# Hand-over from a GRU to an attention-gated GRU: the last weighted sums in feature slices, 16 features stored first

## The chip, the cores and the metric

The kernel runs on one core of one Trainium2 chip, as one program. A core has five engines with instruction streams of their own: TensorE (PE, matrix products), VectorE (DVE), ScalarE (ACT), GpSimd (POOL) and SyncE (SP, which here only issues DMAs). They wait for each other through semaphores. They work on SBUF; PE writes its results to PSUM, which DVE and ACT read too. DRAM is reached through 16 DMA engines. The metric is the device time of one execution in microseconds, median of several runs.

## The reference

For 1024 users with up to 100 past items each (128 numbers an item), the reference runs a GRU over the items, scores every state against a candidate item with a small MLP, and turns the scores into weights with a softmax over time. The weighted sum of the states is `pooled`. Its first 100 of 128 features are then taken, transposed, as attention weights of the 100 steps of a second recurrence, whose state at each user's last step enters a small prediction MLP.

```python
_, gru_seq = jax.lax.scan(gru_step, h0, jnp.swapaxes(item_historical_embedding, 0, 1))
keys = jnp.swapaxes(gru_seq, 0, 1)
...
feat = jnp.concatenate([keys, q, keys - q, q * keys], axis=-1)
score = _mlp(feat, [(att_W0, att_b0), (att_W1, att_b1), (att_W2, att_b2)], jax.nn.relu)
score = jnp.where(mask[:, :, None] == 1, score, -jnp.inf)
attn = jax.nn.softmax(score, axis=1)[..., 0]
pooled = jnp.einsum('bt,btd->bd', attn, keys)
att_seq = pooled.T[:T]
...
    u = a_t[:, None] * u
    h_new = (1.0 - u) * h + u * h_hat
```

So feature 0 of `pooled` weighs step 0 of the second recurrence, feature 1 step 1, and so on: the second recurrence can't take its step 0 before the softmax over all 100 scores is done, and for step t it needs feature t alone.

## The kernel before, in words

**Two phases.** `gru_phase` (from L199) runs the GRU on two halves of 512 users each, states as 128 features x 512 users. `augru_phase` (from L989) runs the second recurrence on the same users, now sorted by the length of their history, so that later steps have fewer columns. There are three builds of the second phase for different spreads of lengths. Between the phases stands a branch: each engine loads a register from `over_d` (L1475) and takes one of two nested `If`s (L1476, L1477). Within a phase the order of each engine's work is the order in which the code is written (`manual_schedule`); the tail of `gru_phase` (L912 to L987) and the head of `augru_phase` (L1396 to L1425) are laid out by hand.

**Attention MLP.** `attend(t)` (L691) scores step t-2 and earlier layers' steps in one go, with products of 32 columns that occupy parts of the array (`pack`, L700). `take(t)` (L724) adds the candidate item's own part `q0` on DVE (L734), applies relu on ACT (L739, or L741 with a bias) and sends the scores through an SBUF-to-SBUF DMA to `s_b` (L746), from which `softmax` transposes them (L786).

**Softmax and weighted sums in blocks.** The softmax is online: the steps are cut into blocks that end at `ENDS`, the last ones 93, 96, 98 and 100. For each block there are scores (L786, L790), maxima (L794 to L800), exponents on ACT (L806) and sums (L809 to L823, with `old` and `den` on L813 and L814). `Half.pool` (L617) then brings `pooled` up to date: it rescales it (L626), multiplies the states `kt` of each step of the block with their weights (L636) and adds the product (L637), at full width of 128 x 512, that is 16 groups of 32 users (`KH`) times 32 features (`R`) on 128 partitions. Half 0's sums run on POOL, half 1's last ones on DVE; the last block's sums run on DVE for both.

**Hand-over.** When the last block is in, DVE multiplies `pooled` with a mask `used` that is 0 where a user's history has ended (L978). The first 32 features go to `pooled_d[0]` in DRAM (L982), the other 96 to `pooled_d[1]` (L987 for half 1, on SP; L1402 for half 0, on ACT's queue). POOL gathers the 32 features back in the order of sorted users (`gather`, L153, four of 128 users for each half). PE transposes the gathered rows into one feature on all partitions (`weight_row`, L1053): feature 0 for `first_state` (L1064, L1065), feature 1 for `first_weights` (ACT copy on L1070). `store_weights` (L1076 to L1079) turns the gathered features into rows in DRAM, from which `load_att` (L1092) reads the later steps' weights.

**Work around it.** The states themselves go to DRAM too (`keys_d`, stored from `kt` on L609) and are gathered back in sorted order by POOL (`load_row`, L188; `gather_early` issues some of them in the GRU phase). `load_key` makes the second recurrence's inputs of steps 0 to 3 from them by transposes on PE (L1110) and ACT copies (L1111). `first_step` computes the gates of step 0 (matmul L1030, sigmoid and tanh L1032), `open_gates` (L1127) the input part of the gates of step 1, `close_gate` (L1131) the state part. In `half_step` follow the sigmoids (L1151, L1152), r times h (L1157), u times its weight (L1165), `rest` (L1168), tanh (L1139), its product (L1155) and the new state (L1159). PE's other work at the end of the GRU phase are the prediction's features (`features`, matmul L667, ACT copy L675, store L677).

The order of the tail just before the branch:

```python
        stage(2)
        exponents()
        stage()
        halves[0].pool(T, nc.gpsimd)
        halves[1].pool(T, nc.vector)
        gather_early(3)
```

The functions that the diff touches:

Of the kernel before, what the change touches and what calls it, by code (L numbers as in the profile page):

```python
# [57 lines left out]
AHEAD = 2  # L58

# [16 lines left out]
FREE_BANK, EARLY_BANKS, LATE_BANKS = 6, (2, 5, 6, 0), (3, 4, 1)  # L76
# [7 lines left out]
def kernel(ctx: ExitStack, tc: tile.TileContext, a: dict, out: bass.AP):  # L84
# [35 lines left out]
    inv_d = dram.tile([B, 2], I32, name="inv_d")  # L120
# [3 lines left out]
        dram.tile([B, n], F32, name=f"pooled_d{j}") for j, n in enumerate((R, P - R))  # L124
# [15 lines left out]
    idx = const.tile([P, GH, NH * 2], I32, name="idx")  # L140
    idx_k = const.tile([P, KH, NH], I32, name="idx_k")
    idx_p = const.tile([P, HB // PR], I32, name="idx_p")
# [8 lines left out]
    def gather(dst, src, g, i):  # L151

        nc.gpsimd.indirect_dma_start(  # L153
            out=dst,
            out_offset=None,
            in_=src,
            in_offset=bass.IndirectOffsetOnAxis(ap=idx[:, g, 2 * i : 2 * i + 1], axis=0),
        )
# [40 lines left out]
    def gru_phase(pools):  # L199
# [72 lines left out]
        def load_later():  # L272
# [31 lines left out]
            ids = pre.tile([P, NG, 2], I32, name="ids")  # L304
# [18 lines left out]
            nc.scalar.copy(own, ids[:, :, 0])  # L323
            room = []
# [114 lines left out]
            place_i = pre.tile([P, KH, NH, 2], I32, name="place_i")  # L439
# [12 lines left out]

            last = pre.tile([P, NK], F32, name="last")
# [31 lines left out]
        class Half:  # L485
# [131 lines left out]
            def pool(self, count, eng):  # L617

                while count and self.todo:
                    e, n, t = self.todo.pop(0)  # L620
                    count -= t is not None
                    acc = pooled[:, self.ks, :]
# [5 lines left out]
                    k = self.kt[t // G][:, :, t % G, :]  # L628
                    if t == 0:
                        eng.tensor_mul(acc, k, w)  # L630
                    else:
                        if psum:
                            d = blocked(banks["kw"])
                        else:
                            d = wp.tile([P, KH, R], F32, tag="kw", name="kw")
                        eng.tensor_mul(d, k, w)  # L636
                        eng.tensor_add(acc, acc, d)  # L637
                    if t is not None and t % G == G - 1:
                        del self.kt[t // G]


# [49 lines left out]
        def attend(t):  # L691
# [17 lines left out]

            for turn in range(2 * NH):  # L710
                i, j = divmod(turn, 2)
                for q in range(2):
                    first(i, q, j)
# [10 lines left out]
        def take(t):  # L724
# [6 lines left out]
            for half in halves:  # L731
                if t < T:
                    sums.append(wp.tile([P, HB], F32, name="f"))
                    nc.vector.tensor_add(sums[-1], p[half.i], q0[:, half.cols])  # L734
            for half in halves:
                half.mv = wp.tile([P, HB], F32, name="mv", bufs=4)
                to, of, bias = half.mv[rows, :], p[half.i][rows, :], bm[half.i][rows, :]
                if t < T:
# [19 lines left out]
        def softmax():  # L758
# [49 lines left out]
            def sums():  # L808
                nc.vector.tensor_mul(e[:, :, :n], e[:, :, :n], on)  # L809
                nc.vector.tensor_reduce(den_n, e[:, :, :n], AX.X, ALU.add)  # L810
                if j:
                    old = sp.tile([P, NK], F32, name="old")
                    nc.vector.tensor_mul(old, den_old, e[:, :, n])  # L813
# [120 lines left out]
        some(2, 3)  # L934
        take(T - 1)
        some(2, 3)
        attend(T)
        some(4)
# [3 lines left out]
        n = ENDS[-3] - ENDS[-4] + 1  # L942
        copy = banks["e"][0][:, : NK * n].rearrange("p (k n) -> p k n", n=n)
        nc.vector.tensor_copy(copy, weights[:, :, :n])
# [4 lines left out]
        halves[0].pool(T, nc.gpsimd)  # L949
        halves[1].pool(1, nc.vector)  # L950
        stage()
        take(T)
        some(4)
        attend(T + 1)
        some(5, 6)
        stage()
        take(T + 1)
        exponents()
        some(5, 6)
        some(7)  # L960
        for half in halves:
            half.store((T - 1) // G)
        halves[1].pool(T, nc.vector)
        stage()
        gather_early(3)
        halves[0].pool(T, nc.gpsimd)
        some(7)
        stage(2)
        exponents()
        stage()  # L970
        halves[0].pool(T, nc.gpsimd)
        halves[1].pool(T, nc.vector)
        gather_early(3)


        for half in reversed(halves):
            t = blocked(s_bs[NH * (soft["j"] % 2) + half.i])
            nc.vector.tensor_mul(t, later["used"][:, half.ks, :], pooled[:, half.ks, :])  # L978
            first, others = (
                d[half.cols, :].rearrange("(k r) (p c) -> p r k c", r=R, c=R) for d in pooled_d  # L980
            )
            nc.sync.dma_start(out=first[0], in_=t[:R])  # L982
            later["att", half.i] = [
# [5 lines left out]
    def augru_phase(pools, widths, alive):  # L989
# [420 lines left out]
        for i in range(NH):  # L1410
            load_key(3, i)
# [137 lines left out]
```

## Time and profile before

| | before |
|---|---|
| median of 3 runs | 2014.82 us (2014.07 to 2015.9) |
| profiled execution, its own time | 2014.8 us |
| span of the profile | 2013.0 us |
| granted TensorE clock, mean | 0.993 |
| PE busy | 1986.5 us |
| DVE busy | 1672.2 us |
| POOL busy | 1277.1 us |
| ACT busy | 935.5 us |
| DMA moved | 204.84 MB, 102 GB/s on average |

The span is the time from the first to the last instruction of the profiled execution, which is one execution and not the median. Busy times add up what each engine did; they overlap. The granted clock is the share of full speed at which TensorE was clocked. In lists of instructions, a number in brackets is the idle time before one, with what ended it; "issue" is time for which the profile shows no releaser. The GRU phase ends, and the second recurrence begins, between about 1376 and 1450 us of the span.

### The profile page before, as it was taken

To read this page: it belongs to the slowest core of one execution; us is meant where nothing else is said; L and a number is where in the kernel's file an instruction comes from. 1 tells how busy PE (TensorE), PEld (TensorE's weight loads), DVE (VectorE), ACT (ScalarE), POOL (GpSimd) and SP (SyncE) were. 2 spreads that over 40 slices of the span, in tenths; PEclk is the share of its full clock that TensorE was granted. 3 is DMA by queue.
4 is the path that set the end of the run, shared out by engine and by line. 5 is a ranking of instruction groups with operands and counts; after the bars stand their busy time and mean duration, and the time that the engine had idled before them with its cause. 6 is when DMAs were issued, how large, how long until landed. Compare 5 with 4: busy or idle time off the path is not lost.

```text
span 2013.0 us, 40935 instructions
## 1 busy us (share of the span) xinstructions
PE 1986.5 (99%) x15324; PEld 992.8 (49%) x15324; DVE 1672.2 (83%) x3017; ACT 935.5 (46%) x1679; POOL 1277.1 (63%) x1325
## 2 busy tenths in 40 slices
PE   9999999999999999999999999998899999999998
PEld 2345555555433333333333333334444556678997
DVE  7878999887978887888878898998487777888985
ACT  4444454454444454444444454453334444445553
POOL 0233939669796959595887868898674354445331
PEclk9999999999999999999999999999899999999998
DMA  4442333323334334333333333333343343333331
GB/s 124 98 117 91 107 103 103 92 83 104 115 112 102 120 107 121 115 112 102 111 98 96 107 104 94 107 96 106 102 127 101 97 110 98 93 105 95 85 78 30
DMA packets 242075, 204.84 MB, mean 102 GB/s; under 512 B 59506, under 2 KB 204890, under 8 KB 241866
## 3 DMA queue, kind: packets, MB, share of 16 engines
q1 hardware_dynamic: 227514, 169.37, 30.1%
q0 software_dynamic: 12480, 32.04, 5.7%
q8 instruction: 122, 2.00, 0.4%
q14 instruction: 87, 0.71, 0.1%
q10 hardware_dynamic: 1872, 0.72, 0.1%
HBM read 146.01 MB, written 54.41 MB: 100 GB/s over the span
## 4 chain that ended last, share of the span: by engine, by line
PE 95%; DVE 3%; issue 1%; ACT 1%; ACTq 0%; DVEq 0%
PE ps L534 49%; PE pm L700 17%; PE pr L1131 4%; PE ph L1131 4%; PE pu L1131 4%; PE pr L1127 4%; PE ph L1127 4%; PE pu L1127 4%; PE pr L1204 0%; PE ph L1204 0%; PE p L1324 0%; DVE pu L1155 0%; PE pu L1030 0%; PE pd L243 0%; DVE ps L564 0%
## 5 line engine op out<-in xcount | busy, mean ns | idle before, releaser
L534 PE MATMUL ps<-x,wih 128*32 128x512 f32 x4800 | 775.9, 593 | 0.0
L534 PE MATMUL ps<-hn,whh 128*32 128x512 f32 x4752 | 769.6, 592 | 1.4 <-ACT hn L582 1.4
L534 PEld LDWEIGHTS ps<-x,wih 128*32 128x32 f32 x4800 | 259.0, 110 | 302.0 <-issue 299.1
L534 PEld LDWEIGHTS ps<-hn,whh 128*32 128x32 f32 x4752 | 257.0, 110 | 298.7 <-issue 294.6
L519 POOL TENSOR_TENSOR xm<-x,m 128x512 f32<-128x512 f32 x200 | 236.7, 1183 | 142.2 <-DMA m<-mask_d 82.5
L546 ACT ACTIVATE r<-ps,brz 128x512 f32<-128x512 f32 x200 | 137.5, 688 | 388.4 <-PE ps L534 388.2
L520 POOL TENSOR_TENSOR hist<-hist,xm 128x512 f32<-128x512 f32 x200 | 257.9, 1289 | 15.7
L700 PE MATMUL pm<-hn,wk 128*32 128x512 f32 x1200 | 266.4, 592 | 0.1
L700 PE MATMUL pm<-kq,wkq 128*32 128x512 f32 x1200 | 265.8, 592 | 0.0
L188 POOL DMA_INDIRECT rows<-keys_d,idx_k x218 | 211.4, 970 | 81.4 <-POOL rows L187 46.7
L637 POOL TENSOR_TENSOR pooled<-pooled,kw 128x512 f32<-128x512 f32 x191 | 246.0, 1288 | 15.0
L636 POOL TENSOR_TENSOR kw<-kt,e 128x512 f32<-128x512 f32 x191 | 206.3, 1080 | 70.7 <-DVE e L809 70.6
L565 ACT ACTIVATE ps<-ps,bih 128x512 f32<-128x512 f32 x200 | 132.4, 662 | 225.9 <-DVE ps L564 225.9
L554 DVE SCALAR_TENSOR_TENSOR u<-ps,bhh,r 128x512 f32<-128x512 f32 x198 | 147.6, 746 | 73.2 <-PE ps L534 70.5
L1139 ACT ACTIVATE c<-ph,bh 128x510 f32<-128x510 f32 (+57 forms) x174 | 88.1, 507 | 258.8 <-PE ph L1131 221.3
L700 PE MATMUL pm<-mv,w 128*32 128x512 f32 (+1 forms) x808 | 196.3, 592 | 0.8 <-DVE e L790 0.8
L569 DVE TENSOR_TENSOR d<-hn,ps 128x512 f32<-128x512 f32 x198 | 136.1, 687 | 35.9 <-ACT ps L565 35.5
L570 DVE TENSOR_TENSOR d<-ps,d 128x512 f32<-128x512 f32 x200 | 138.3, 692 | 28.4 <-ACT ps L566 14.0
L187 POOL COPY rows<-rest 128x1 f32<-128x1 f32 x202 | 38.3, 190 | 193.0 <-DVE rest L1168 182.9
L582 ACT COPY hn<-ps 128x512 f32<-128x512 f32 x200 | 116.4, 582 | 92.8 <-DVE kq L576 91.0
L564 DVE TENSOR_TENSOR ps<-ps,u 128x512 f32<-128x512 f32 x200 | 140.0, 700 | 22.4 <-PE ps L534 1.5
L571 DVE TENSOR_TENSOR ps<-ps,d 128x512 f32<-128x512 f32 x200 | 139.9, 699 | 6.8
(228 smaller groups left out, 3120.4 us busy)
## 6 DMA issues: line engine op xcount, KB each, us to landing
x<-in_hist_x SPq DMA_DIRECT2D x210, 256.0 KB
keys_d<-kt SPq DMA_DIRECT2D x48, 1024.0 KB
m<-mask_d SPq DMA_DIRECT2D x200, 128.0 KB
rows<-keys_d,idx_k POOLq DMA_INDIRECT x218
s_b<-mv SPq DMA_DIRECT2D x200, 8.0 KB
keys_d<-kt SPq DMA_DIRECT2D x32, 64.0 KB
mask_i<-in_mask SPq DMA_DIRECT2D x8, 200.0 KB
part_d<-part SPq DMA_DIRECT2D x2, 400.0 KB
```

The source lines that it names most:

```text
L188: nc.gpsimd.indirect_dma_start(out=r[:, at, :], out_offset=None, in_=keys_d[q], in_offset=bass.IndirectOffsetOnAxis(ap=idx_k[:, k, i : i + ...
L519: nc.gpsimd.tensor_mul(d, x, m)
L520: nc.gpsimd.tensor_add(acc, acc, d)
L534: nc.tensor.matmul(p[ts(q, R), :], lhsT=w[:, g, ts(q, R)], rhs=v, start=(j == 0), stop=(j == len(parts) - 1),)
L554: nc.vector.scalar_tensor_tensor(out=u, in0=ph, scalar=bhh[:, 2:3], in1=r, op0=ALU.add, op1=ALU.mult,)
L564: nc.vector.tensor_add(pi, pi, u)
L571: nc.vector.tensor_add(pi, pi, d)
L636: eng.tensor_mul(d, k, w)
L637: eng.tensor_add(acc, acc, d)
L700: nc.tensor.matmul(p[i][s, :], lhsT=w[:, s], rhs=v, start=start, stop=stop)
L1127: nc.tensor.matmul(p, lhsT=m[:, 1, :], rhs=k, start=True, stop=False)
L1131: nc.tensor.matmul(p, lhsT=m[:, 0, :], rhs=v, start=False, stop=True)
```

## The change

`SOON = R // 2 = 16` is new: `pooled_d[0]` holds 16 features instead of 32, `pooled_d[1]` 112 instead of 96. The parts are:

1. The last block's sums (and, for half 1, those of the block before) are made in two slices, features 0 to 15 (`soon`) and 16 to 31 (`rest`), on all partitions. The `soon` slices come first, half 0's on POOL with one product on DVE (`product`), half 1's on DVE. They are stored at once from `pooled`, unmasked, half 1 by SP and half 0 by ACT's queue. Then DVE makes the `rest` slices of both halves and the multiplication with `used`.
2. The other 112 features are stored by SP in step 2 of the second recurrence, by four DMAs for each half.
3. The mask for the 16 early features is applied after the gather: a third column of `inv_d` carries each user's length in sorted order, `used_s` is made from it, and `first_state` multiplies 15 gathered features with it.
4. The keys of steps 0 and 1 and the gates of step 0 are made before the branch. The gates lie in `item` and in tiles of `s_b`, and the keys of step 0 and 1 in `h_all` and `hist`; the pool `fp3` goes. The keys of steps 2 and 3 are made within steps 1 and 2.
5. For the last two GRU steps the candidate item's part is added by PE, with six more products in each `attend` (`query`), and `take` reads PSUM directly.
6. For one softmax block the weights and `old` lie in PSUM while the sums are made (`soft["copy"]`).
7. In step 1 the copy of feature 1 (`first_weights`) stands behind the sigmoids.
8. The store of the last states to `keys_d` stands later on SP: behind the copies of scores for the last step and behind the second feature store. 13 rows of `keys_d` are gathered early instead of 14.

The diff, cut to its core:

```diff
+SOON = R // 2
...
-        dram.tile([B, n], F32, name=f"pooled_d{j}") for j, n in enumerate((R, P - R))
+        dram.tile([B, n], F32, name=f"pooled_d{j}") for j, n in enumerate((SOON, P - SOON))
...
-            def pool(self, count, eng):
+            def pool(self, count, eng, cs=slice(0, R)):
...
-                    acc = pooled[:, self.ks, :]
+                    acc = pooled[:, self.ks, cs]
+                    if n is None:
+                        eng.tensor_add(acc, acc, e)
+                        continue
...
+            def product(self, cs):
+
+                e, n, t = self.todo.pop()
+                d = wp.tile([P, KH, R], F32, tag="kw", name="kw")[:, :, cs]
+                w = e[1][:, self.ks, n].unsqueeze(2).to_broadcast(d.shape)
+                nc.vector.tensor_mul(d, self.kt[t // G][:, :, t % G, cs], w)
+                self.todo.append((d, None, t))
...
+            def query(i, *groups):
+                for q in groups:
+                    pack(i, q, wq[i], item[:, halves[i].cols], False, False)
+
             for turn in range(2 * NH):
                 i, j = divmod(turn, 2)
+                if j and T - 2 <= t < T:
+                    query(i, 0, 1)
+                    if i:
+                        query(1, QB[1])
+                        query(0, QB[0])
...
-                if t < T:
+                if t < T - 2:
...
+                f, old = e, None
+                if banks and both[1] is None:
+                    b = banks["e"][0]
+                    f = soft["copy"] = b[:, : NK * rows].rearrange("p (k n) -> p k n", n=rows)
+                    old = b[:, HB - NK :]
+                    nc.vector.tensor_copy(f, e[:, :, :rows])
+                nc.vector.tensor_reduce(den_n, f[:, :, :n], AX.X, ALU.add)
...
+        halves[0].pool(T, nc.gpsimd)
+        gather_early(2)
+        soon, rest = slice(0, SOON), slice(SOON, R)
+        late = [[], list(halves[1].todo)]
+        halves[1].pool(T, nc.vector, soon)
+        some(6, 7)
+        for half in halves:
+            key(1, half)
         for half in halves:
             half.store((T - 1) // G)
-        halves[1].pool(T, nc.vector)
-        stage()
-        gather_early(3)
-        halves[0].pool(T, nc.gpsimd)
-        some(7)
         stage(2)
         exponents()
...
         stage()
-        halves[0].pool(T, nc.gpsimd)
-        halves[1].pool(T, nc.vector)
+        for half in halves:
+            late[half.i] += half.todo
+        halves[0].product(soon)
+        halves[0].pool(T, nc.gpsimd, soon)
+        halves[1].pool(T, nc.vector, soon)
         gather_early(3)
-
-
+        for half, eng in zip(reversed(halves), (nc.sync, nc.scalar)):
+            eng.dma_start(
+                out=pooled_d[0][half.cols, :].rearrange("(k r) c -> r k c", r=R),
+                in_=pooled[:R, half.ks, soon],
+            )
         for half in reversed(halves):
+            half.todo = late[half.i]
+            half.pool(T, nc.vector, rest)
             t = blocked(s_bs[NH * (soft["j"] % 2) + half.i])
             nc.vector.tensor_mul(t, later["used"][:, half.ks, :], pooled[:, half.ks, :])
...
-                gather(r[:, g, :R], pooled_d[0], g, i)
+                gather(r[:, g, :SOON], pooled_d[0], g, i)
...
             nc.vector.tensor_mul(h3[i], p, h)
+            r = sorted_rows[i][:, :, 1:SOON]
+            nc.vector.tensor_mul(r, r, used_s[:, i, :, 1:])
...
-            if t == 1 and i == 0:
-                store_weights(0, pa.tile([P, HB], F32, tag="a", name="pw"))
-                first_state(1, spare)
-            elif t == 1:
-                first_weights(1, spare)
+            if t == 1:
+                first_weights(i, spare)
+                load_key(2, i)
...
             if t == 1 and i:
                 store_weights(1, spare)
+                load_key(3, 0)
+            elif t == 1:
+                open_state(1, 0)
+                store_weights(0, pa.tile([P, HB], F32, tag="a", name="pw"))
+                first_state(1, spare)
+            elif t == 2 and i == 0:
+                load_key(3, 1)
...
-        for i in range(NH):
-            load_key(0, i, (None, FREE_BANK)[i])
-        gates = [first_step(i) for i in range(NH)]
-        for i in range(NH):
-            load_key(1, i, (FREE_BANK, None)[i])
-        for to, t in later["att", 0]:
-            nc.scalar.dma_start(out=to, in_=t)
+        gates = [later["gates", i] for i in range(NH)]
+        keys.update({(1, i): later["key", 1, i] for i in range(NH)})
         sorted_rows = [gather_weights(i) for i in range(NH)]
-        for k in range(14, KH):
+        for k in range(13, KH):
             load_row(1, 0, k)
...
         open_gates(1, 1, EARLY_BANKS)
         open_gates(1, 0, LATE_BANKS)
...
-        first_weights(0, spare)
...
+                if t == FIRST[1] - 2:
+                    for to, of in later["att", i]:
+                        nc.sync.dma_start(out=to, in_=of)
```

## The prediction

> **What bounds the kernel now.** I read the busy totals and the chain that ended last first, then one table by stage. PE is busy 99% of the span and holds 95% of the chain, so a change away from PE's few pauses is worth nothing.
>
> ```profile
> span 2013.0 us, 40935 instructions
> PE 1986.5 (99%) x15324; PEld 992.8 (49%) x15324; DVE 1672.2 (83%) x3017; ACT 935.5 (46%) x1679; POOL 1277.1 (63%) x1325
> PE 95%; DVE 3%; issue 1%; ACT 1%; ACTq 0%; DVEq 0%
> ```
>
> The stage table (stretch, its length, busy time of PE, PEld, DVE, ACT, POOL, granted clock, DMA share, GB/s) shows where the pauses are.
>
> ```profile
> 1385.00:1400.00 15.00, 13.84 (x77) 8.51 (x70) 11.89 (x27) 7.44 (x16) 11.21 (x11) 1.00 0.25 78
> 1400.00:1420.00 20.00, 11.47 (x39) 6.37 (x38) 14.81 (x36) 6.73 (x11) 15.84 (x15) 0.74 0.63 170
> 1420.00:1440.00 20.00, 15.46 (x58) 8.10 (x57) 5.83 (x9) 4.72 (x8) 9.69 (x11) 0.92 0.19 40
> 1440.00:1460.00 20.00, 20.00 (x57) 9.66 (x56) 12.85 (x21) 7.89 (x12) 15.86 (x28) 0.99 0.62 185
> ```
>
> Here the GRU hands over to the second recurrence: PE stands idle 14 us in 55, and its clock drops to 0.74. All the edits lie between about 1376 and 1450. The timelines of DVE, POOL, ACT and PE (start, duration, instruction, idle before it and who ended it) give the links:
>
> ```profile
> 1388.35 1.29 DVE L734 TENSOR_TENSOR f<-pm,q 128x512 f32<-128x512 f32 x2 [2.55 <-PE pm L700]
> 1392.25 1.29 DVE L814 TENSOR_TENSOR den<-den,old 128x32 f32<-128x32 f32 x1
> 1402.27 0.19 DVE L814 TENSOR_TENSOR den<-last,old 128x32 f32<-128x32 f32 x1
> 1407.73 0.68 DVE L626 TENSOR_TENSOR pooled<-pooled,last 128x512 f32<-128x512 f32 x1
> 1414.71 1.29 DVE L978 TENSOR_TENSOR s_b<-used,pooled 128x512 f32<-128x512 uint8 x2
> 1429.23 0.70 DVE L1064 TENSOR_TENSOR first<-first,first_u 128x512 f32<-128x512 f32 x1 [13.22 <-PE first L1053]
> ...
> 1420.67 0.95 POOL L153 DMA_INDIRECT att_r<-pooled_d,idx  x1 [2.51 <-DMA pooled_d<-s_b]
> 1424.44 0.95 POOL L153 DMA_INDIRECT att_r<-pooled_d,idx  x1 [0.30 <-issue]
> ...
> 1432.73 0.58 ACT L1070 COPY at<-spare 128x512 f32<-128x512 f32 x1 [4.96 <-PE pu L1131]
> 1434.80 0.66 ACT L1151 ACTIVATE pr<-pr,br 128x510 f32<-128x510 f32 x1 [1.48 <-PE spare L1053]
> ...
> 1407.44 1.94 PE L1110 MATMUL pk<-ident,rows 128*128 128x128 f32 x8 [6.32 <-issue]
> 1427.83 1.16 PE L1053 MATMUL first<-ident,att_r 128*128 128x128 f32 x8 [0.72 <-issue]
> 1438.15 2.07 PE L1131 MATMUL pr<-h_all,wr 128*128 128x510 f32 x2 [0.37 <-DVE h_all L1065]
> ```
>
> The order is: last weighted sums on DVE until 1414.71, mask multiply until 1416.0, store, first gather 1420.67 (4.67 us after), fourth gather 1424.44, `first` at 1427.83, then step 1 with more waits. PE, before and after `first`, does what is there.
>
> [...] `pu<-k,wu` at 1411.16 takes 2.08 us where its like at 1420.05 takes 1.02, and the change comes after 5.2 us of work. [...] L814 takes 1.29 us at 1392.25, and 0.19 where one input lies in PSUM. [...]
>
> **The change part by part.** Times are in the clock of the profiled execution of before.
>
> *Query on PE for the last two GRU steps.* Four column groups work side by side; each holds four attend passes of 0.857 us (3.43 together, as from 1376.16 to 1379.59). Six extra passes make the fullest group six: 5.14, so +1.71 us twice. attend(98) ends at 1381.3 instead of 1379.59, two features (2.90) bring 1384.2, and attend(99) ends at E = 1389.4 to 1389.6 instead of 1387.24; its pauses of 1.3 us for `mv` go, since the `f` add on DVE (2x1.2) is gone. E is later by about 2.2 us.
>
> *DVE up to the last block's weights.* Gone: both pairs of `f` adds, and 2.31 - 0.4 = 1.9 us of L813/L814 through operands in PSUM. The full-width ops that stood behind them then fit before E + 3.0, when the scores return (store to `s_b` 1.66 to 2 us, plus relu). From there: two transposes and tops 3.05, exponents and sums 1.4, the other transposes 1.1, one half-width block of five ops 2.13, the next tops 3.05, and exp on ACT behind the key copies to about E + 15; sums, reciprocal and product end at X = E + 16.95 = 1406.5, against 1407.73. So 1.2 us of gain survive; the rest went into the later E.
>
> *Last sums in feature slices.* A full DVE op is 0.69 us and its 346-wide like 0.516, a slope of 1.06 ns an element: 256 wide is 0.42, and a block of five 2.13 instead of 3.48. After X: half 0's product 0.33, half 1's soon part 2.13, its rest (two blocks) 4.26, multiply 0.6, half 0's rest 2.13, multiply 0.7: 10.15 us, end at 1416.6. Before: 8.3 us, end at 1416.0. The full work is done once either way, in more and shorter instructions.
>
> *Early store and gather.* The store of half 1 could leave at X + 2.5 = 1409, half 0's after POOL's four half ops (2.4) at about E + 19.5 = 1409. But in the built program the first weight gather waits for DVE's last mask multiply: its tile takes memory that `used` held. PE's open_gates waits for the last rest op too (a PSUM bank). So the gather starts not behind the store but behind all the rest: 1416.6 + 0.1 = 1416.7, against 1420.67. What is saved is the landing and the POOL branch, 4.0 us. POOL itself (five full ops 5.75, two gathers 2.5, four half ops 2.4, three gathers 3.8, branch at most 2.5) is ready by E + 25.8 = 1415.3. One more rows gather (13 early instead of 14) follows the weights, with no one waiting.
>
> *Key stores moved.* 2 MB to keys_d now stand on SP directly in front of the pooled_d0 store. They take 264 to 360 GB/s in windows of 2 us of before, so with the other traffic 2.4 MB at 310 GB/s: 7.8 us from E + 16, drained at E + 24; the 16-feature store lands at E + 24.5 to 25 = 1414.5. The gather waits until 1416.7 anyway: cover of 2 us, cost nothing. Gone, it costs its lateness in full. The 112-feature store leaves at step 2; what hides it is the time until the later weights are gathered, well past step 15.
>
> *Keys and gates ahead of the branch.* Keys 0 and 1 and the four first gates run on PE while it waits for DVE, instead of 1407.44 to 1420. Before, open_gates (five us at full clock) ended at 1425.2 and keys 3 at 1427.1. Now it starts with DVE's last rest op at 1415.9, after some 8 us of idle[...]: six pairs of matmuls take 6.9 to 7.7 us, and event waits 0.7, ending 1423.5 to 1424.3. The fourth gather is issued at 1416.7 + 4.7 and lands two us later: 1423.4. Both meet, so `first` starts at 1423.7 to 1424.3 against 1427.83: -3.5 to -4.1 us.
>
> *From `first` to the steady steps.* ACT's copy of `at` (idle 4.96 before it, 1.48 after) comes behind the sigmoids, which frees 1.7 us on ACT; keys 2 and 3 transposed in steps 1 and 2 put four times 0.45 us on a busy PE. Walking both chains, ph of half 1 in step 1 comes 16.75 us after `first` instead of 17.0: -0.25.
>
> Sum: I take 1423.7[...]: -4.13 - 0.25 = -4.4, or a span of 2008.6 instead of 2013.0. The profiled execution was 2014.8 and the median 2014.82, so the same difference applies: **2010.5 us**. Own range of this case 2009 to 2012.
>
> **Rivals.** (a) *Slower: cold PE through step 1.* It speaks for it that PE now has idle stretches of 8 us before open_gates, and that the warm-up in before ran on gates that have moved away. If the pauses of step 1 keep the clock at half, the six gate pairs take 10.3 us, which puts `first` at 1426.6 (-1.2), and the eight matmul pairs of step 1 cost 0.86 us more each, of which some 5.5 us fall on the chain: +4.3, or 2019.1. [...] A pooled_d0 store that lands after 1421 behind the keys would have the same sign. (b) *Void part: ACT's stall stays or PE's extra 3.4 us delay E by more.* Before's DVE saw attend(99) 1.1 us after PE's modelled end; if that repeats E is 1390.5 and all behind it 1.0 later, and if ACT's 1.7 us do not come, step 1 costs 1.45 (the moved keys) instead of giving 0.25: -4.13 + 1.0 + 1.45 = -1.7, or 2013.1. (c) *More gain: clock high.* If the features and gates ahead keep the clock, open_gates ends at 1421.5, the gathers set `first` at 1423.4 (-4.4), and the half-clock pieces of step 1 in before (1.54 and 2.07 us instead of 1.02 at 1436.23 and 1438.15) give 1.5 more: -6.1, or 2008.7. That the gather is tied to the store, and goes before the rest, as the code's order suggests, would be more still; the built waits exclude it.
>
> **How the numbers follow.** Forecast 0.48, (c) 0.20, (b) 0.20, (a) 0.12. A difference of 0.2% (4.0 us) is about what a measurement of this kernel can tell from no change, so faster means below 2010.8, slower above 2018.8 (nearly all of (a)'s tail is counted there). Forecast lies on the bound: 0.33 of its 0.48 below, and all of (c): 0.53 faster; the rest of it and (b), 0.35 same; 0.12 slower. The range 2007.5 to 2014.5 holds nearly all of the forecast, (b) and (c), and leaves (a) and the outer tails out.
>
> **What would show it.** POOL's first gather near 1416.7, its releaser DVE's multiply and not a DMA; the DVE end near 1416.6; L813/L814 at 0.2 us in the first softmax; `first` near 1424 with half-clock gates ahead of it; ACT without the 4.96 us wait. Wrong if the gather follows a DMA landing later, if the clock stays low through step 1, or if E is later than 1390.5.

## The result, and the profile after

The changed kernel takes 2012.72 us (median of 14 runs, 2011.0 to 2015.82), the kernel before 2014.85 (14 runs, 2012.94 to 2016.83). The ratio is 0.9991, with a 95% interval of 0.9984 to 0.9998: about 2 us faster, where 4.3 were forecast. That holds for one chip: on another the order was the other way round, 2005.12 us before and 2007.45 after ("Second profiles" below). The profiled execution took 2012.06 us, its span is 2010.3.

First the totals and the chain that ended last, then the stage table (stretch, its length, busy time of PE, PEld, DVE, ACT, POOL, granted clock, DMA share, GB/s), all of the changed kernel:

```profile
span 2010.3 us, 40989 instructions
PE 1987.7 (99%) x15348; PEld 1198.2 (60%) x15348; DVE 1673.9 (83%) x3033; ACT 936.0 (47%) x1681; POOL 1273.8 (63%) x1325
PE 96%; DVE 1%; DMA 1%; issue 0%; ACT 0%; POOL 0%; SPq 0%; DVEq 0%; POOLq 0%; ACTq 0%
```

```profile
1385.00:1400.00 15.00, 15.00 (x90) 10.00 (x83) 13.68 (x38) 7.27 (x17) 13.23 (x13) 1.00 0.16 51
1400.00:1420.00 20.00, 13.93 (x35) 6.56 (x34) 11.74 (x33) 5.36 (x9) 12.20 (x15) 0.83 0.62 168
1420.00:1440.00 20.00, 15.52 (x58) 9.47 (x58) 9.07 (x15) 5.57 (x9) 12.11 (x17) 0.83 0.28 77
```

PE's pauses between 1385 and 1440 shrink from 14.2 to 10.6 us. But in 1420 to 1440 PE is no busier than before (15.52 against 15.46) at a lower clock (0.83 against 0.92). The gain lies before that stretch and part of it is lost within. The timelines of DVE, POOL, SP and PE (start, duration, instruction, idle before it and its releaser) show where:

```profile
1386.31 0.19 DVE L853 TENSOR_TENSOR den<-den,last 128x32 f32<-128x32 f32 x1
1404.27 0.41 DVE L662 TENSOR_TENSOR kw<-kt,last 128x256 f32<-128x256 f32 x1
1413.81 0.69 DVE L1056 TENSOR_TENSOR s_b<-used,pooled 128x512 f32<-128x512 uint8 x1
1422.53 0.70 DVE L1122 TENSOR_TENSOR first<-first,item 128x512 f32<-128x512 f32 x1 [8.03 <-PE first L1111]
1426.87 0.69 DVE L1217 TENSOR_TENSOR r<-h_all,pr 128x510 f32<-128x510 f32 x1 [2.79 <-issue]
1433.66 0.69 DVE L1123 TENSOR_TENSOR h_all<-spare,s_b 128x512 f32<-128x512 f32 x1
...
1415.87 0.95 POOL L155 DMA_INDIRECT att_r<-pooled_d,idx  x1 [4.57 <-DMA pooled_d<-pooled]
...
1406.75 3.54 SPq L1048 DMA_DIRECT2D pooled_d<-pooled  x1
...
1410.66 2.04 PE L1187 MATMUL pr<-hist,wr 128*128 128x510 f32 x2 [5.15 <-DVE last L652]
1421.90 0.49 PE L1111 MATMUL first<-ident,att_r 128*128 128x128 f32 x2 [0.72 <-DMA att_r<-pooled_d,idx]
1424.01 2.07 PE L1191 MATMUL pr<-h_all,wr 128*128 128x510 f32 x2 [1.62 <-DVE h_all L1123]
```

The start of the kernel differs by up to 2.7 us between executions of the same program, so stages are counted from the first product of attend(98) (1375.17 before, 1373.71 after). The two columns "again" are second profiles, taken on another chip, and are discussed below.

| us after attend(98) starts | before | before, again | after | after, again |
|---|---|---|---|---|
| attend(99) ends on PE | 12.07 | 12.05 | 13.50 | 13.50 |
| copy of the last block's weights ends | 32.64 | 31.62 | 30.64 | 30.48 |
| DVE's last mask multiply ends | 40.83 | 39.81 | 40.79 | 40.61 |
| first weight gather starts | 45.50 | 43.60 | 42.16 | 42.18 |
| DVE's first product of `first` | 54.06 | 52.12 | 48.82 | 48.94 |
| fourth tanh of the second recurrence | 80.94 | 75.38 | 78.97 | 78.34 |

From before to after, the first product comes 5.24 us earlier, but the way from there to the fourth tanh takes 30.15 us instead of 26.88. The difference, 1.97 us, is near what the timed runs show (2.13).

### The profile page after: what moved, and what is told of

Read it like the earlier page. It is cut to its first block, busy times and chain, and to the rows that moved or that the text cites. A ratio compares the mean times of both kernels' runs of the same rounds, so it can differ in the third digit from the quotient of the medians.

```text
span 2010.3 us, 40989 instructions
## 1 busy us (share of the span) xinstructions
PE 1987.7 (99%) x15348; PEld 1198.2 (60%) x15348; DVE 1673.9 (83%) x3033; ACT 936.0 (47%) x1681; POOL 1273.8 (63%) x1325
## 4 chain that ended last, share of the span: by engine, by line
PE 96%; DVE 1%; DMA 1%; issue 0%; ACT 0%; POOL 0%; SPq 0%; DVEq 0%; POOLq 0%; ACTq 0%
PE ps L547 51%; PE pm L723 18%; PE ph L1191 4%; PE pr L1191 4%; PE pu L1191 4%; PE pu L1187 4%; PE ph L1187 4%; PE pr L1187 4%; DMA rows<-keys_d,idx_k 1%; PE last L690 1%; PE pr L1269 0%; DMA item<-in_item 0%; PE ph L1269 0%; PE p L1389 0%; DVE pu L1215 0%
## 5 line engine op out<-in xcount | busy, mean ns | idle before, releaser
L547 PE MATMUL ps<-x,wih 128*32 128x512 f32 x4800 | 712.5, 593 | 0.0
L547 PE MATMUL ps<-hn,whh 128*32 128x512 f32 x4752 | 705.9, 592 | 1.3 <-ACT hn L595 1.3
L547 PEld LDWEIGHTS ps<-x,wih 128*32 128x32 f32 x4800 | 301.9, 110 | 225.7 <-issue 39.7
L547 PEld LDWEIGHTS ps<-hn,whh 128*32 128x32 f32 x4752 | 299.5, 110 | 222.5 <-issue 35.5
L653 POOL TENSOR_TENSOR pooled<-pooled,kw 128x512 f32<-128x512 f32 (+1 forms) x190 | 243.7, 1283 | 14.9
L652 POOL TENSOR_TENSOR kw<-kt,e 128x512 f32<-128x512 f32 (+1 forms) x190 | 205.6, 1082 | 67.9 <-DVE e L841 67.9
L723 PE MATMUL pm<-hn,wk 128*32 128x512 f32 x1200 | 245.5, 592 | 0.6 <-issue 0.6
L723 PE MATMUL pm<-kq,wkq 128*32 128x512 f32 x1200 | 245.5, 592 | 0.0
```

The lines of the kernel that those rows point to most:

```text
L547: nc.tensor.matmul(p[ts(q, R), :], lhsT=w[:, g, ts(q, R)], rhs=v, start=(j == 0), stop=(j == len(parts) - 1),)
L723: nc.tensor.matmul(p[i][s, :], lhsT=w[:, s], rhs=v, start=start, stop=stop)
```

## The experiments

Times are set against runs of the kernel before on the same chip, since it did not take the same time on all: 2013.13, 2011.58 and 2005.12 us in the three sets. Stages of profiles from different chips are compared with each other; the two profiles of the changed kernel differ by up to 0.2 us until the first product and by 0.6 at the fourth tanh.

**Is it the landing of the 16-feature store that holds the gather?** As I read the built program, POOL's first gather waits, in the branch that runs, for both stores to pooled_d0 and not for DVE; the run with early keys below bears that out. SP's issue of half 1's store takes 3.54 us at 1406.75, right behind 2 MB for keys_d. The DMA view of the changed kernel for 1413 to 1415 (packets, then each queue with packets, MB and share) still shows small packets on q1, of 64 bytes each by the store's pattern:

```profile
DMA packets 269, 0.09 MB, mean 46 GB/s; under 512 B 244, under 2 KB 252, under 8 KB 268
q1 hardware_dynamic: 230, 0.02, 9.3%
```

Counted in shorter windows, half 1's small packets begin at about 38.5 us after the start of attend(98), when the 2 MB ahead of them on the queue are through, and end at about 40.6; the gather follows at 42.2. Four runs try whether that is cause or coincidence. The first moves the key stores behind the early stores:

```diff
-        for half in halves:
-            half.store((T - 1) // G)
         stage(2)
...
                 in_=pooled[:R, half.ks, soon],
             )
+        for half in halves:
+            half.store((T - 1) // G)
```

> The changed kernel with one edit: the two 1 MB stores of the last states to keys_d are issued on SP behind the two pooled_d0 stores instead of in front of them. Theory 1 (landing): in the branch that runs, the first weight gather waits only for the two 32 KB stores, and half 1's lands at about 1415 because 2 MB stand in front of it on SP's queue. Then the gather starts where POOL's own branch lets it, 2.5 us after its last rows gather instead of 4.57, that is 2.1 us earlier; DVE's first product comes 1.5 to 2.1 us earlier and the kernel is 1.5 to 2 us faster (ratio to before 0.9981). Rival (POOL's branch or DVE's last multiply bound it): the idle time before the first weight gather stays at 4.2 to 4.6 us and the time stays within 0.5 us of the changed kernel.

Measured: 2012.77 us, ratio to before 0.9995 (0.9986 to 1.0003). The gather did not start earlier but later, at 42.91. POOL's timeline:

```profile
1415.79 0.95 POOL L155 DMA_INDIRECT att_r<-pooled_d,idx  x1 [5.46 <-DMA rows<-keys_d,idx_k]
```

SP's issue fell from 3.54 to 0.34 us and half 1's small packets were through by 35 us. But now half 0's store, issued by ACT, took longer: its 528 small packets (on q10) lay between 36.0 and 40.1 us, while the key packets were passing too, where they had taken from 37.6 to 39.7 in the changed kernel. The theory as I had put it, one queue and its order, is refuted. That the last landing counts, whichever store it is, fits but is not shown by this run: the gather comes 2.8 us after the last small packet, where it comes 1.2 to 1.9 us after it in the changed kernel and in the late-store runs below, and the profile names a gather of rows, some of whose packets passed as late as 42.5 us. The second run moves the key stores the other way:

```diff
         take(T + 1)
+        for half in halves:
+            half.store((T - 1) // G)
         some(4, 5)
...
-        for half in halves:
-            half.store((T - 1) // G)
         stage(2)
```

> The changed kernel with one edit: the two 1 MB stores to keys_d are issued on SP right behind the last copy of scores, some 4 us earlier, as in the kernel before. Theory 1 (landing): the 512 packets of 64 bytes of half 1's weight store are last seen 41 us after the start of attend(98) because 2 MB stand in front of them; now they are through by 37 us, and the first weight gather starts where POOL's branch lets it, at 40 us instead of 42.2, and DVE's first product comes 1 to 1.6 us earlier; time 1 to 1.5 us better than the changed kernel. Rival: the keys' traffic delays the scores of the last step or the features and with them the last softmax, which comes 0.5 us or more later, and the gain is gone.

Measured: 2006.96 us, ratio to before 0.9977 (0.9970 to 0.9984), on a chip where before took 2011.58. SP, POOL and DVE in its timelines:

```profile
1405.17 0.33 SPq L1048 DMA_DIRECT2D pooled_d<-pooled  x1
...
1411.50 0.95 POOL L155 DMA_INDIRECT att_r<-pooled_d,idx  x1 [1.77 <-DMA rows<-keys_d,idx_k]
...
1412.22 0.69 DVE L1056 TENSOR_TENSOR s_b<-used,pooled 128x512 f32<-128x512 uint8 x1
```

Both stores' small packets are through by 36 us, the gather starts at 39.23 (2.9 earlier than in the changed kernel), the first product at 46.55 (2.3 earlier), the fourth tanh at 76.69 (2.3 earlier). The last softmax copy is where it was (30.50). The gather now starts 0.72 us before DVE's last mask multiply, so it does not wait for it. Theory 1 held at these stages, with more than its figures. The changed kernel itself was not run on this chip, so the gain in time over it is not measured.

The third and fourth undo the early store, in the changed kernel and in the one with early key stores. Each half's features are stored from the masked tile, behind its rest sums:

```diff
-        for half, eng in zip(reversed(halves), (nc.sync, nc.scalar)):
-            eng.dma_start(
...
             nc.vector.tensor_mul(t, later["used"][:, half.ks, :], pooled[:, half.ks, :])
+            (nc.sync if half.i else nc.scalar).dma_start(
+                out=pooled_d[0][half.cols, :].rearrange("(k r) c -> r k c", r=R),
+                in_=t[:R, :, soon],
+            )
```

> The changed kernel with the early store undone: each half's 16 features are stored from the masked tile, so only when its rest sums and its mask multiply are done; everything else stays. Theory 1 (landing behind the keys): in the changed kernel the early store of half 1 lands only 41 us after the start of attend(98) because of the 2 MB in front of it, so the early start is mostly wasted: the late store (DVE's end is at 40.8, half 0's store lands at about 43) costs just 1.5 to 2.5 us at the first weight gather (43.5 to 44.5 instead of 42.2) and 1 to 2 us of time. Rival (the early store is worth the whole 5.8 us by which it is issued ahead of DVE's end): 4 us or more.

> The same undoing of the early store, with the key stores moved early as in the run that did that alone. There the first weight gather started at 39.2 us and DVE's first product at 46.6. Now the store can't land before about 43, so the gather starts at 43.5 to 44.5 and the first product 4 to 5 us later than in that run; the time is 3 to 4.5 us worse than there. Rival (the gain of that run came from relief of DMA traffic alone, not from an earlier landing): within 1 us of it.

Measured, on one chip with the changed kernel again (2007.45 us, 20 runs): 2009.32 us with the late store, 2009.58 with late store and early keys. The gathers start at 44.21 and 44.12, the first products come at 51.15 and 51.07:

```profile
1417.06 0.95 POOL L155 DMA_INDIRECT att_r<-pooled_d,idx  x1 [6.79 <-DMA pooled_d<-s_b]
```

```profile
1417.12 0.95 POOL L155 DMA_INDIRECT att_r<-pooled_d,idx  x1 [6.70 <-DMA pooled_d<-s_b]
```

With a late store it makes no difference where the keys stand (0.09 us at the gather, 0.26 us in the time). So the gain of the early keys is not relief of DMA traffic: it is the earlier landing. And the early store, as it was made, is worth 2.0 us at the gather and 1.9 us of time; with the keys out of its way it is worth 4.9 us at the gather (44.12 against 39.23, profiles of two chips).

The place of the key stores also moves PE's pause at the branch. The first product of open_gates with the keys behind, and with early keys:

```profile
1406.04 1.09 PE L1187 MATMUL pr<-hist,wr 128*128 128x510 f32 x2 [1.51 <-DVE pooled L653]
...
1407.20 1.09 PE L1187 MATMUL pr<-hist,wr 128*128 128x510 f32 x2 [3.27 <-DVE pooled L653]
```

PE's pause is 1.51 us in the one, 3.27 to 3.60 in the three runs with early keys, and 4.50 to 5.17 in the seven profiles with the keys where the changed kernel has them. In all 14 profiles PE's first product behind the branch starts 1.51 to 1.65 us after a packet of 16 KB on q8 has passed (1.59 us in the profile of before, 1.57 in that of the changed kernel), a queue that the DMA view calls "instruction". What PE waited for there, and why the packet comes later in some orders than in others, is not shown.

**Is it POOL's branch?** The three rows gathers ahead of the branch go behind the weights:

```diff
         halves[1].pool(T, nc.vector, soon)
-        gather_early(3)
...
-        for k in range(13, KH):
+        for k in range(10, KH):
```

> The changed kernel with one edit: the three rows gathers that POOL issues ahead of the branch are issued behind the eight weight gathers (10 early instead of 13). Theory 1 (landing): POOL reaches its wait 3.8 us earlier and waits 3.8 us longer, the first weight gather stays at about 11.5 us behind the last softmax copy, nothing changes in the time (within 0.5 us), unless step 4's rows come too late. Rival (POOL's branch): the gather starts 3.8 us earlier, and the time falls by about 2 us.

Measured: the first weight gather starts 11.53 us after the last softmax copy, as before this edit (11.52), though POOL had been idle 8.24 us. POOL's branch does not hold it. But the time rose to 2022.01 us (4 runs, ratio 1.0041, 1.0026 to 1.0057), which neither theory had. The DVE timeline shows where:

```profile
1440.03 0.68 DVE L1137 COPY att_t<-pw 16x512 f32<-16x512 f32 x1 [9.58 <-remote]
```

Its operand `pw` was complete on PE at 1432.94 by the profile. But the profile models when PE's products end, and the trace also records each semaphore event, the signals for which engines wait. PE's signals stop at 1431.51 and go on at 1437.14, 1438.57 and 1440.00, and the copy starts 0.03 us after the last of these. So DVE waited for a signal of PE that came about 7 us after the modelled end. Whether PE's products were late or only their signals, and why, is left open.

**Does the query on PE pay?**

```diff
-                if j and T - 2 <= t < T:
+                if False:
...
-                if t < T - 2:
+                if t < T:
```

> The changed kernel with one edit: the six extra products in each of the last two attends are taken out and the candidate's part is added on DVE again, as before. Theory 1 (the query pays): PE's two attends shrink by 1.7 us each, but DVE gets its two pairs of additions back (2.4 us) ahead of and inside the first softmax; the last softmax copy comes 0.5 to 1.5 us later and the kernel is 0.5 to 1.5 us slower than the changed one. Rival (PE's 3.4 us sit on the chain): the last softmax copy comes about 2 us earlier, and the kernel is 1 to 2 us faster.

Measured: 2013.91 us, ratio 1.0005 (0.9997 to 1.0013). attend(99) ends at 12.35 us instead of 13.50, but the last softmax copy comes at 33.18 instead of 30.64, the fourth tanh at 81.15 instead of 78.97. By these stages the query is worth 2.2 to 2.5 us, more than either theory gave it. The two profiles are of different chips, and the changed kernel was not timed on this one.

**Step 1: the clock, the order, or ACT?** First PE is kept busy while it waits for the gathers, with products into a bank that is overwritten next:

```diff
-        def weight_row(t, i, p):
+        def weight_row(t, i, p, turn=None):

             for g in range(GH):
+                if turn:
+                    turn(P)
+                    turn(P)
...
-        def first_state(i, p):
-            weight_row(0, i, p)
+        def first_state(i, p, turn=None):
+            weight_row(0, i, p, turn)
+            for _ in range(3 if turn else 0):
+                turn(2 * P)
...
```

> The changed kernel with one edit: while PE waits for the gathered weights, it makes products that nobody reads (two of 128 columns ahead of each of the four transposes of first, three of 256 behind them) into the bank that is overwritten next. Theory 1 (clock): step 1 takes 18.4 us from DVE's first product to the second half's ph because PE runs at half clock from 1424 to 1430; kept busy, pr and pu of step 1 take 1.02 us instead of 2.07 and 1.91, and the stretch shrinks by 2 to 3 us (ratio to before 0.998). Rival (order): the loss comes from what stands ahead of ph on PE (eight transposes for the weights and four for key 2) and from ACT's late copy; then pr and pu are short but the stretch shrinks by under 1 us, or the extra products delay first by what the clock gives back.

Measured: 2014.13 us, ratio 1.0009 (1.0000 to 1.0017). PE and ACT in its timelines:

```profile
1422.58 1.12 PE L1196 MATMUL pr<-h_all,wr 128*128 128x510 f32 x2 [0.89 <-issue]
1423.54 1.02 PE L1196 MATMUL pu<-h_all,wu 128*128 128x510 f32 x2
...
1426.03 0.66 ACT L1216 ACTIVATE pr<-pr,br 128x510 f32<-128x510 f32 x1 [21.86 <-PE pk L1175]
```

The products run at full clock now, 1.12 us instead of 2.07. But ACT takes `pr` up only at 1426.03, 2.3 us after its modelled end and 0.08 us after a signal of PE at 1425.95: a late signal again. The way from the first product to the first tanh grows from 8.95 to 9.44 us, that to the fourth from 30.15 to 33.42. Since late signals fell into the stretch, the run does not say what the half clock costs alone.

Then half 1's first state is put ahead of key 2:

```diff
             if t == 1:
                 first_weights(i, spare)
-                load_key(2, i)
+                if i:
+                    load_key(2, i)
+                else:
+                    first_state(1, pa.tile([P, HB], F32, tag="a", name="first"))
...
                 store_weights(0, pa.tile([P, HB], F32, tag="a", name="pw"))
-                first_state(1, spare)
+                load_key(2, 0)
```

> The changed kernel with one edit in step 1: half 1's first state (its eight transposes on PE and its two products on DVE) is put directly behind half 0's copy of feature 1, and half 0's key of step 2 behind the row store, so that the state of half 1 no longer waits for the copies of feature 1 and key 2 on ACT. Theory 1 (order of step 1): between half 0's r (1426.87) and half 1's state (1434.36) the changed kernel takes 7.5 us where before took 2.6, because the transposes stand behind key 2 and two copies in the same banks; the stretch then shrinks by 2 to 3 us, and the time by 1 to 2.5 us against the changed kernel (ratio to before 0.9985 or less). Rival (PE's half clock or late gathers set it): the stretch from DVE's first product to the fourth tanh shrinks by under 0.7 us and the time stays.

> The changed kernel with both edits, the key stores early and half 1's first state early. If both places are on the chain, their gains add up: the fourth tanh comes 3 to 4.5 us earlier after the start of attend(98) than in the changed kernel, and the ratio to before is 0.997 or less. If only one of them is on the chain, the result is that of the better one alone.

Measured: 2012.58 us (ratio 1.0004, 0.9998 to 1.0011), and with early keys as well 2009.00 (0.9989, 0.9982 to 0.9995), where early keys alone had 2006.96 on the same chip. Half 1's state is complete 10.0 us after the first product instead of 11.8, but the second tanh comes 21.82 us after it instead of 19.50: key 2 now waits for the bank that the row store empties. PE's timeline of the run with that edit alone:

```profile
1432.07 0.60 PE L1136 MATMUL pw<-ident,att_r 128*16 128x128 f32 x4 [2.08 <-DVE att_r L1125]
1434.02 0.93 PE L1170 MATMUL pk<-ident,rows 128*128 128x128 f32 x4 [1.36 <-DVE att_t L1138]
```

A wait took the place of the one removed; the expected 1 to 2.5 us did not come. With early keys as well the second tanh comes 19.76 us after the first product, where early keys alone had 19.49, so there too nothing is gained.

Last, the late copy of feature 1 alone, in the kernel before:

```diff
-        first_weights(0, spare)
...
             if t == 1 and i == 0:
+                first_weights(0, spare)
                 store_weights(0, pa.tile([P, HB], F32, tag="a", name="pw"))
                 first_state(1, spare)
```

> The kernel before with one part of the change alone: half 0's copy of feature 1 stands behind the two sigmoids of step 1 on ACT, and its transposes behind the state products on PE. The prediction has it free 1.7 us on ACT: r of half 0 comes 1.5 to 2 us earlier after DVE's first product, ph of half 0 too, and the kernel is about 1 us faster than before (0.9995). Rival [...]: the sigmoid starts no earlier than 5 us after DVE's first product, and the time is that of before within 0.5 us.

Measured: 2011.70 us against 2011.58, ratio 1.0004 (0.9995 to 1.0012). The expected gain is not there. r of half 0 does come earlier, 3.3 us after the first product instead of 6.3, but it comes after 3.3 us in the second profile of before too, without this edit. Half 1's state, which needs the bank that the copy frees, is complete after 8.94 us (8.86 before). The fourth tanh, at 79.26 us against 80.94, would have suggested a gain of 1.7 us that the times do not show.

**Second profiles.** Both kernels once more, on another chip:

> The changed kernel once more, for a second profile: if the stages are steady, gather at 42.2 +- 0.3, first product at 48.8 +- 0.5 and fourth tanh at 79.0 +- 0.7 us after the start of attend(98).

> The kernel before once more, for a second profile: if the stages are steady, gather at 45.5 +- 0.5, first product at 54.1 +- 0.7 and fourth tanh at 80.9 +- 0.7 us after the start of attend(98); if the fourth tanh comes near 79.3, the gain seen with half 0's late copy of feature 1 is no gain.

Measured: the changed kernel's stages repeat within 0.7 us (last column of the table). The kernel before does not: its fourth tanh comes at 75.38 instead of 80.94, and it takes 2005.12 us (median of the set's 40 runs) where the changed one takes 2007.45 (20 runs). On this chip the change is slower, ratio 1.0012 (1.0006 to 1.0019). Before is 1.0 us earlier there at the last softmax copy already and 1.9 at the gather, so the change gains 3.18 us up to the first product instead of 5.24, and loses 6.14 us after it instead of 3.27. PE's and ACT's timelines of before there, and PE's line in the first profile of before:

```profile
1424.30 1.06 PE L1053 MATMUL spare<-ident,att_r 128*128 128x128 f32 x8
1425.40 0.58 ACT L1070 COPY at<-spare 128x512 f32<-128x512 f32 x1 [2.14 <-PE spare L1053]
1427.24 0.66 ACT L1151 ACTIVATE pr<-pr,br 128x510 f32<-128x510 f32 x1 [1.26 <-PE pr L1131]
...
1428.82 1.06 PE L1053 MATMUL spare<-ident,att_r 128*128 128x128 f32 x8
```

Here the copy starts 0.04 us after its operand (`spare`, 1424.30 + 1.06 on PE). In the first profile the modelled end of the operand is 1429.88 and the copy starts at 1432.73, 2.85 us later. The semaphore events of that trace say why: PE's signal comes at 1432.71, and its next nine signals come together, between 1434.77 and 1435.10; the sigmoid starts at 1434.80. So ACT's 4.96 and 1.48 us of idle time were waits for late signals of PE, and no cost of the order in the code. In the second profile the stretches that follow are shorter too: half 1's state is complete 6.25 us after the first product instead of 8.86, PE's clock stays at 1.00 from 1420 to 1440, and the second tanh comes 13.05 us after the first product instead of 16.67.

In the four profiles on this chip all but at most one of PE's signals are on record, and between 1390 and 1450 us none comes over 0.1 us after the modelled ends. In each of the ten other profiles some come later than that in step 1, and 154 to 192 of about 2240 are not on record. Whether this makes the difference in time between the chips, and whether the recording itself has a part in it, is not shown; early keys took 2006.96 us on a chip with late signals.

## Why the prediction was right or wrong

The time was inside the range of 2007.5 to 2014.5 and the direction right on the chip of the result. But the size was half of the forecast, outside the narrower range of 2009 to 2012, and it came about as a sum of two errors that went against each other, which is luck. The number is nearly that of rival (b), 2013.1, by another sum.

- **Query on PE.** Forecast: E, the end of attend(99), 2.2 us later. Measured: 1.43. Each attend takes about 5.3 us, near the 5.14 worked out. The second grew by 0.55 us, with its pauses gone, but the first by 0.90 instead of 1.71, because its passes ran partly beside the last GRU products.
- **DVE up to the last weights.** Forecast 1.2 us earlier (31.3 us after the start of attend(98)), measured 2.0 (30.64). L853 takes 0.19 us as expected, beside POOL's product at 1386.29. (The prediction's own example at 1402.27 stands where POOL was idle; the like at 1406.64, beside a product on POOL, takes 0.19 us too. The runs show 0.19 us with an operand in PSUM against 1.29 us at 1392.25, and not what makes the difference.)
- **Sums in slices.** Forecast 10.15 us from the last copy to DVE's end, measured 1404.35 to 1414.50, that is 10.15. "The full work is done once either way" holds for both engines together only: in the kernel before, half 0's last block ran on POOL (1408.67 to 1414.50 in its timeline, not on DVE as stated at the top), and its second slice is new on DVE.
- **Early store and gather.** The start was near (41.5 us after attend(98) forecast, 42.16 measured) for the wrong reason. The step that failed is "in the built program the first weight gather waits for DVE's last mask multiply". With early keys the gather starts before that multiply, so the program does not hold it there. (As I read the built program, the wait stands in one of the three builds of the second phase, and not in the one that runs.) The gather follows the landing of the stores, and the step that then counts is the price of the moved key stores, put at "cost nothing": half 1's store landed at about 40.6, not at 39, with no cover from DVE. By its own sign, "its releaser DVE's multiply and not a DMA", the prediction failed here. What came true is what rival (c) named and excluded, a gather tied to the store, together with rival (a)'s late landing behind the keys, at a smaller price.
- **Gates.** open_gates was to start with DVE's last rest op (40.7 us); it started at 36.95, after 5.15 us of pause at the branch, at half clock for 5.2 us (2.04, 1.91 and 1.91 us for its first three pairs, 1.02 for its last two), as long as in the profile of before. The shorter stretch on which the forecast's 1423.7 rested was my estimate. So the wait for the last rest op did not hold its start. With the keys behind, where PE came earlier, its last pair did wait 1.76 us for DVE's rest op. It was done by 45.2, and `first` was bound by the gathers alone: 5.24 us of gain at the first product instead of 3.5 to 4.1.
- **From `first` to the steady steps.** Forecast -0.25 up to ph of half 1, measured +3.27 up to the fourth tanh (+2.83 up to that ph, both counted from DVE's first product). This is the step that was off most. It rested on ACT's idle 4.96 and 1.48 us in before, read as a cost of the order in the code. They were waits for late signals of PE; the second profile of before has the copy without them, and late copying alone gained nothing. What the changed order costs against an undisturbed step 1 shows on the other chip: 29.40 us from the first product to the fourth tanh against 23.26. Three things lie in it, seen but not priced apart: PE's products at half clock (2.07 and 1.91 us, a granted clock of 0.50 from 1424 to 1430), half 1's state behind key 2 and two copies (complete 11.07 us after the first product against 6.25), and the keys' transposes on PE (0.85 us once at half clock, 0.44 three times).
- **Chances.** Rival (b), ACT's gain that doesn't come, is what happened in step 1; rival (c)'s earlier `first` happened too. Rival (a), PE cold into step 1, is seen in the clock (0.50 from 1424 to 1430), but its price is not settled.

In these profiles open_gates runs at half clock after pauses of 4.50 us and more (2.04 us for its first pair of products after 5.15 us in the changed kernel), and at full clock after those of up to 3.60 us (1.09 us after 3.27 with early keys, 1.09 after 1.51 with the keys behind). In the changed kernel the granted clock is 0.50 from 1410 to 1416 and 1.00 again from 1417. The drop in step 1 is less simple: no single pause ahead of `pr` at 1424.01 is longer than 1.62 us, but PE was busy for only 1.7 of the 5.1 us before it. What sets the clock in either place is not shown, and what made PE's signals late in the other profiles I can't say. Packets on the two queues that the DMA view calls "instruction" do not account for ACT's wait in the first profile of before: none passes there between 1422.9 and 1432.3.

No run takes the slices, the keys and gates ahead of the branch, or the operands in PSUM out alone, so what each of these is worth is not shown.

## What to carry to other kernels

In these runs a small store on which the critical path waits landed late with big ones near it, on its own queue (packets gone at 40.6 us instead of 34.2) and on another one (4.1 us for its packets instead of 2.1). Move the big one well ahead (here the gather came 2.9 us earlier), and judge by when the small packets are gone, not by when the store was issued. When a program has branches, take wait lists from the branch that runs. Before an idle time is priced as the cost of an order, compare the start of the waiting instruction with the end of its operand; if they differ, look for the signal that the instruction waited for. Such a pause may belong to that execution alone (2.85 us in the first profile of before, 0.04 in the second), and a second profile on another chip is worth more than a longer sum.

The best version of these runs is the changed kernel with early key stores: 0.9977 (0.9970 to 0.9984) of before on one chip. On the chip where the kernel before was undisturbed it was not run.

## What the runs showed that I had not expected

- The same kernel before takes 2014.85 us in one set and 2005.12 in another. Of the 10.2 us between the two profiles' spans, 2.7 lie ahead of attend(98), 5.6 between it and the fourth tanh, and the rest later.
- The same store of 32 KB took 3.54 us to issue right behind 2 MB on its queue, and 0.33 us with the early keys.
- PE's signals came late in step 1 of some profiles, and other engines then waited although their operands were complete by the profile's modelled ends: ACT 2.85 us in one profile of before, ACT 2.3 us in the kept-warm kernel, DVE 7.1 us with three rows gathers more behind the weights.
